# A four-layer graph network: node stages in pairs behind the sums, later hand-overs, the MLP bias by a matmul

## Chip, cores and metric

The kernel runs on one core of a Trainium2 chip. The metric is the device time of one execution in microseconds (us); the median of ten is compared. Engines: PE (TensorE matmuls), PEld (its weight loads), DVE (VectorE), ACT (ScalarE), POOL (GpSimd), SP (SyncE, here only a DMA queue).

## What is computed

A graph of 6250 nodes of 128 features and 100,000 edges (`src`, `dst`) goes through four layers, each on `relu(layernorm(x))`, added to `x`. Cut from the reference:

```python
def layer0(x, ...):                      # attention of 8 heads
    x = layernorm(x) * ln_gamma + ln_beta
    x = x @ W_in + b_in
    e = leaky((x @ W_u + b_u)[src] + (x @ W_v)[dst])
    probs = softmax of e over the edges of one dst
    return segment_sum(x.reshape(n, 16, 8)[src] * probs, dst) @ W_ff + b_ff
def layer1(x, W, b, gamma, beta):        # graph convolution, self loops
    out = segment_sum((x @ W)[src] * dinv[src] * dinv[dst], dst) + b
    return relu(batchnorm over the nodes of out)
def layer2(x, ...):                      # two attention layers of one head, self loops, relu between
    h = x @ W
    e = leaky((h @ a_src)[src] + (h @ a_dst)[dst])
    return segment_sum(h[src] * softmax(e), dst) + bias
def layer3(x, rbf, d_gamma, ...):        # pairs
    w = silu(rbf @ rad_W1 + b) @ rad_W2 + b + silu(d_gamma @ sph_W1 + b) @ sph_W2 + b
    alpha = sum over a head of q[dst-side] * w * k / sqrt(32), times two edge weights
    return segment_sum(alpha * v[...], src)
```

## The kernel before

`survey` sorts the nodes by degree and puts them into 49 blocks (`NR`) of 128; block `b` has room for `CAPS[b]` edges a node (44, 25, 24 ... 9; 820 in all, `TC`). A stage of a layer fetches, for each block, `CAPS[b]` columns: each is one indirect DMA that POOL issues (`fetch`, L1577), 128 rows of a table in HBM, one to a partition. Row tiles have three buffers. Then the block is scored, multiplied and summed on DVE, and the sums go through PE as nodes: transposed, copied by ACT, multiplied with a weight, and written by SP into the table of the next layer. A layer's first gather needs the last of these writes.

From line L1559 on the order on each engine is the order in which the program issues (a manual schedule); nothing is reordered, and an instruction that waits holds all behind it on its engine. The order comes from generators: each `yield` ends a hop, and `in_turns` steps all live blocks once a turn, the older first. A block starts with its gathers, then has `turns_of(b)` turns, about one for 4.5 gathers and at least 4. After each turn `behind` gives background generators a step when their `Pace` says so (a rate per column of `CAPS`):

- layer 0 (`block0`, stage g0): `source_ranks` (the place of each edge's source, 5 columns a step) and `edge_weights` (the MLP of layer 3 over all edges, 200 groups of 500 edges, two hops each: L1236 adds its bias from PSUM and SBUF);
- layer 1 (`part1`): `source_places` (a counting sort, with the scan L1397), and `edge_weights` further; then the batch norm's sums and `blocks1`, 17 groups of three blocks, with no gathers;
- layer 2 (`block2`, stages g2 and g3): the rest of `edge_weights`, then `source_rows` (the rest of the sort: L1447 and L1449 on DVE, L1441 on PE, L1433 on ACT, L1429 on DVE).

The DVE lines of a block: in g0 L1594 to L1598 (scores), L1603 (rows times weights, both in SBUF), L1605 (sum), L1606 to L1609; in g2 and g3 L1745 to L1748, L1753, L1755, L1756 to L1758. The nodes of g0 follow in the same generator: `times_in_hops` with `wf`, L1614 and L1615, `norm_in_hops` (L1045 to L1057), `times_in_hops` with `w1`, L1619. In g3 L1770, the norm, one `times_in_hops` (L1774 and L1775 take it up), then `pair_rows`: POOL fetches the block's edge rows (`pr_e`, L1792, two buffers), DVE multiplies them (L1797, both in SBUF), SP writes them out with `v` (L1801, L1802). `fast_pairs` is the last stage.

Of the kernel before, what the change touches and what calls it, by code (L numbers as in the profile page):

```python
# [842 lines left out]
def survey(k, dst):  # L843
# [9 lines left out]
    with tc.tile_pool(name="sv", bufs=1) as p:  # L853
# [99 lines left out]
        nc.vector.tensor_copy(k.rank_b, rl)  # L953
# [119 lines left out]
def times_in_hops(k, p, ps, h, w, width, got):  # L1073
# [3 lines left out]
    t = ps.tile([128, 512], F32, name="th_p").rearrange("p (b d) -> p b d", b=4)  # L1077
    for b in range(nb):
        nc.tensor.transpose(t[:, b, :], h[:, b, :], k.ident)
    yield  # L1080
# [3 lines left out]
    y = ps.tile([128, 512], F32, name="th_p")  # L1084
# [3 lines left out]
    yield  # L1088
# [102 lines left out]
def edge_weights(k, c, ps, m, bias, attr32, attr4, ew1, ew2):  # L1191
# [39 lines left out]
    def outputs(y, out, n, v):  # L1231

        if v == 0:
            nc.scalar.copy(out[:, :, D:D + 2], scale[:, n * KC:(n + 1) * KC, None].to_broadcast([EP, KC, 2]))
        o = out.rearrange("p (u v) f -> p u v f", v=4)[:, :, v, 0:D]
        nc.vector.tensor_tensor(o, y[:EP].rearrange("p (u d) -> p u d", u=4), bias[:EP, None, :].to_broadcast([EP, 4, D]), op=ALU.add)  # L1236
        if v == 3:
            at = n * KC * (D + 2)
            by_engines(nc.sync.dma_start, to[:, at:at + KC * (D + 2)], out.rearrange("p c f -> p (c f)"))
# [5 lines left out]
    yield  # L1245
    aT = keep(t, 0)
    yield
    t = turn(0, 1)
    yield
    dT = keep(t, 1)  # L1250
    yield
    load(1)
    out = after = None
    g = y = last = None
    for n in range(EC // KC + 1):
        for v in range(4 if n < EC // KC else 1):

            if g is not None:
                y = ps.tile([128, 512], F32, name="ew_y")
                for u in range(4):  # L1260
                    e = slice(u * EP, (u + 1) * EP)
                    nc.tensor.matmul(y[:EP, u * D:(u + 1) * D], lhsT=g[:, 0, e], rhs=m.r2, start=True, stop=False)  # L1262
                    nc.tensor.matmul(y[:EP, u * D:(u + 1) * D], lhsT=g[:, 1, e], rhs=m.s2, start=False, stop=True)  # L1263
            h = None
            if n < EC // KC:
                h = ps.tile([D, 2, 512], F32, name="ew_h")
                nc.tensor.matmul(h[:, 0, 0:4 * EP], lhsT=m.r1[:, v, :], rhs=aT, start=True, stop=True)
                nc.tensor.matmul(h[:, 1, 0:4 * EP], lhsT=m.s1[:, v, :], rhs=dT, start=True, stop=True)
            t = None
            if v in (1, 2) and n + 1 < EC // KC:  # L1270
                t = turn(n + 1, v - 1)
            yield

            gone = last
            if h is not None:
                g = c.tile([D, 2, 4 * EP], F32, name="ew_g", bufs=2)
                for i, first in enumerate((m.b1, m.c1)):
                    nc.scalar.activation(g[:, i, :], h[:, i, 0:4 * EP], AF.Silu, bias=first)  # L1278
            if t is not None:
                new = keep(t, v - 1)  # L1280
                if v == 1:
                    after = new
            if gone is not None:
                if gone[1] == 0:
                    out = c.tile([EP, KC, D + 2], F32, name="ew_out", bufs=2)
                outputs(y, out, *gone)
            last = n, v
            if v == 3:
                aT, dT = after, new
                if n % 2:  # L1290
                    load(n // 2 + 2)
            yield


def source_ranks(k, c, ps):

    nc, tc = k.nc, k.tc
    KC = 5  # L1300
    lanes = k.dram.tile([TC, 128], BF16, name="src_lanes")
# [107 lines left out]
def source_rows(k, c, ps):  # L1409
# [17 lines left out]
    for c0 in range(0, TC + 4 * KS_, KS_):  # L1427
# [8 lines left out]
        for cc, t, l in waiting:  # L1436
            if cc % KG == 0:
                acc = ps.tile([128, 2, 512], F32, name="sr_acc", bufs=2)
# [519 lines left out]
```

## Time and profile before

| what | us |
|---|---|
| median of 10 runs | 6430.18 (6423.03 to 6433.51) |
| the profiled execution | 6431.29, its span 6429.4 |
| POOL, DVE, PE, ACT busy in the span | 4524.6, 4019.6, 2821.1, 1176.2 |
| g0: first gather's start to last gather's end | 450.8 to 1618.0 |
| layer 1's gathers | 1636.4 to 2696.7 |
| g2's gathers | 2777.4 to 3900.7 |
| g3's gathers | 3914.8 to 5163.6 |
| the pairs' gathers and output | 5213.8 to 6425 |
| one gather on POOL: shortest, and idle time behind it | 0.94, 0.30 |

The times of the stages are read from POOL's timeline. A group's row gives busy time and the mean of one instruction, then the idle time of the engine in front of it and what ended it; "issue" there means that the engine waited for nothing the profile shows. An indirect DMA's time on POOL is that of making it, not that of the transfer.

### The profile page before, as it was taken

How to read it: one execution, taken by the hardware profiler on the slowest of the kernel's cores; microseconds unless marked ns; L12 is line 12 of the kernel's file. 1: busy time of each engine (PE TensorE's matmuls, PEld its weight loads, DVE VectorE, ACT ScalarE, POOL GpSimd, SP SyncE). 2: the span in 40 equal slices, each digit the busy share in tenths (PEclk: the TensorE clock that was granted, in tenths of full speed). 3: DMA queues.
4: the chain of work that ended last, by engine and by line, in shares of the span. 5: the costliest groups of instructions: out<-in, count | busy, mean ns of one | idle time of the engine just before them, and what ended most of it. 6: DMA issues, size and time to landing. Idle time of an engine off the chain costs nothing. (4 is left out here: it accounts for less than half of the span.)

```text
span 6429.4 us, 45921 instructions
## 1 busy us (share of the span) xinstructions
PE 2821.1 (44%) x13096; PEld 1851.5 (29%) x13096; DVE 4019.6 (63%) x7548; ACT 1176.2 (18%) x2275; POOL 4524.6 (70%) x4403
## 2 busy tenths in 40 slices
PE   2321444444445456444443443323333136666666
PEld 2211333333223334333321111011111035555555
DVE  9746778885438733443447786667787445555555
ACT  0111233334111111122210010111222211111111
POOL 0047777777677777557777777777777757777776
PEclk9755666766666677666666666656666568888888
DMA  0125334443322223232222223867778853333343
GB/s 6 51 53 87 95 95 104 102 104 81 76 76 73 81 86 92 59 78 78 75 72 50 51 52 47 184 158 178 181 177 183 182 137 100 100 100 101 100 101 91
DMA packets 456941, 626.12 MB, mean 97 GB/s; under 512 B 83151, under 2 KB 357874, under 8 KB 446835
## 3 DMA queue, kind: packets, MB, share of 16 engines
q0 software_dynamic: 159296, 397.56, 25.4%
q1 hardware_dynamic: 297009, 224.87, 15.2%
q8 instruction: 110, 1.80, 0.1%
q14 instruction: 162, 1.33, 0.1%
q10 hardware_dynamic: 364, 0.57, 0.0%
HBM read 441.86 MB, written 180.80 MB: 97 GB/s over the span
## 5 line engine op out<-in xcount | busy, mean ns | idle before, releaser
L1818 POOL DMA_INDIRECT fp_rows<-pair_rows,ids x882 | 863.5, 979 | 288.2 <-issue 201.9
L1577 POOL DMA_INDIRECT g_x<-l2b_t,ranks x776 | 874.4, 1127 | 254.7 <-issue 217.1
L1577 POOL DMA_INDIRECT g_x<-l_t,ranks x820 | 810.4, 988 | 268.1 <-issue 258.7
L1577 POOL DMA_INDIRECT g_x<-l2a_t,ranks x776 | 832.0, 1072 | 236.4 <-issue 227.5
L1577 POOL DMA_INDIRECT g_x<-l_t,ell x776 | 812.6, 1047 | 238.3 <-issue 229.5
L1441 PE MATMUL sr_acc<-sr_t,sr_l 128*128 128x441 f16 x1640 | 527.7, 469 | 987.2 <-DVE sr_l L1449 983.3
L1262 PE MATMUL ew_y<-ew_r,ew_g 128*125 128x128 f32 x1600 | 461.5, 384 | 721.2 <-DVE ew_out L1236 355.3
L1262 PEld LDWEIGHTS ew_y<-ew_r,ew_g 128*125 128x125 f32 x1600 | 365.5, 281 | 787.0 <-ACT ew_g L1278 475.8
L1441 PEld LDWEIGHTS <-sr_l 128*128 128x128 f16 x1640 | 160.3, 116 | 1332.5 <-DVE sr_l L1449 1205.4
L1823 DVE TENSOR_TENSOR fp_oh<-iota_l,fp_rows 128x384 f32<-128x384 f32 x294 | 164.3, 559 | 496.1 <-DMA fp_rows<-pair_rows,ids 495.5
L1849 PE MATMUL fp_acc<-fp_rows,fp_oh 128*128 128x128 f32 x1764 | 333.2, 336 | 280.1 <-DVE fp_rows L1843 279.5
L1263 PE MATMUL ew_y<-ew_s,ew_g 128*125 128x128 f32 x1600 | 451.0, 378 | 5.3
L1656 DVE TENSOR_REDUCE g_s<-g_x 128x128 f32<-128x2432 f32 (+16 forms) x50 | 183.3, 3666 | 382.4 <-DMA g_x<-l_t,ranks 382.4
L1755 DVE TENSOR_REDUCE g_a<-g_x 128x128 f32<-128x2048 f32 (+13 forms) x96 | 389.0, 4052 | 3.3
L1447 DVE TENSOR_SCALAR sr_t<-sr_it,sp_tile 128x882 f16<-128x882 f16 x820 | 383.7, 468 | 0.0
L1263 PEld LDWEIGHTS ew_y<-ew_s,ew_g 128*125 128x125 f32 x1600 | 367.7, 283 | 20.9 <-ACT ew_g L1278 17.8
L1849 PEld LDWEIGHTS fp_acc<-fp_rows,fp_oh 128*128 128x128 f32 x1764 | 271.1, 230 | 353.8 <-DVE fp_rows L1843 353.5
L1797 DVE TENSOR_TENSOR pr_e<-pr_e,pr_kv 128x2432 f32<-128x2432 f32 (+16 forms) x50 | 117.4, 2349 | 353.1 <-issue 178.0
L1831 ACT COPY fp_ot<-fp_tr 128x384 f32<-128x384 f32 x294 | 140.9, 479 | 1071.2 <-PE fp_tr L1828 1062.9
L1835 PE MATMUL fp_qe<-own,fp_ot 128*128 128x128 f32 x1764 | 311.7, 326 | 0.0
L1449 DVE TENSOR_SCALAR sr_l<-sr_it,sp_lane,sr_w 128x128 f16<-128x128 f16 x820 | 299.3, 365 | 11.0 <-POOL sr_w L1419 11.0
L1835 PEld LDWEIGHTS fp_qe<-own,fp_ot 128*128 128x128 f32 x1764 | 286.1, 241 | 0.0
(310 smaller groups left out, 6102.9 us busy)
## 6 DMA issues: line engine op xcount, KB each, us to landing
edge_rows<-ew_out SPq DMA_DIRECT2D x50, 910.0 KB
rk_row<-src_lanes SPq DMA_DIRECT2D x164, 160.0 KB
fp_rows<-pair_rows,ids POOLq DMA_INDIRECT x882
g_x<-l_t,ranks POOLq DMA_INDIRECT x820
g_x<-l_t,ell POOLq DMA_INDIRECT x776
g_x<-l2a_t,ranks POOLq DMA_INDIRECT x776
g_x<-l2b_t,ranks POOLq DMA_INDIRECT x776
ew_a<-in_edge_attr_dram SPq DMA_DIRECT2D x25, 448.0 KB
```

The lines of the kernel that those rows point to most:

```text
L1262: nc.tensor.matmul(y[:EP, u * D:(u + 1) * D], lhsT=g[:, 0, e], rhs=m.r2, start=True, stop=False)
L1263: nc.tensor.matmul(y[:EP, u * D:(u + 1) * D], lhsT=g[:, 1, e], rhs=m.s2, start=False, stop=True)
L1441: nc.tensor.matmul(acc[:, h, 0:HT], lhsT=l, rhs=t[:, h * HT:(h + 1) * HT], start=(cc % KG == 0), stop=end)
L1447: nc.vector.tensor_scalar(t, it, k.tile3[:, cc:cc + 1], None, op0=ALU.is_equal)
L1449: nc.vector.tensor_scalar(l, it[:, 0:128], k.lane3[:, cc:cc + 1], weight[:, cc % KG:cc % KG + 1], op0=ALU.is_equal, op1=ALU.mult)
L1577: nc.gpsimd.indirect_dma_start(out=rows[:, j, :], out_offset=None, in_=table, in_offset=bass.IndirectOffsetOnAxis(ap=ids[:, at:at + 1], ax ...
L1656: nc.vector.tensor_reduce(s, rows[:, :n, :].rearrange("p w d -> p d w"), axis=AX.X, op=ALU.add)
L1755: nc.vector.tensor_reduce(a, v.rearrange("p w d -> p d w"), axis=AX.X, op=ALU.add)
L1818: nc.gpsimd.indirect_dma_start(out=rows[:, t, :], out_offset=None, in_=k.pairs, in_offset=bass.IndirectOffsetOnAxis(ap=k.ids[:, at:at + 1] ...
L1823: nc.vector.tensor_tensor(oh, k.iota_l[:, None, :].to_broadcast([128, TG, 128]), rows[:, :, D + 1:D + 2].to_broadcast([128, TG, 128]), op= ...
L1835: nc.tensor.matmul(qe[:, t, :], lhsT=ot[:, t, :], rhs=k.own[:, h, 0:D], start=True, stop=True)
L1849: nc.tensor.matmul(acc, lhsT=oh[:, t, :], rhs=rows[:, t, D + 2:2 * D + 2], start=(t0 + t == 0), stop=(t0 + t == TB - 1))
```

## The change

- `edge_weights`: the bias enters the PSUM sum by a matmul with a row of ones, and ACT copies the result out. One hop a group instead of two; within a hop first ACT's work on what PE made in the hop before, then PE's.
- `source_ranks`: ten columns a group instead of five, and the high part of a rank is stored times 128, so that PE sums both parts and one column a rank comes out; a group takes two hops, each result is taken up later.
- `source_rows`: the matmuls are issued in the step that makes their operands; groups of 15.
- `times_in_hops` may wait two turns instead of one behind each of PE's parts, and use one PSUM tile for both.
- `in_turns` has a second list, `tails`, stepped after the live blocks. The node part of a block becomes a generator of its own that goes there: in g0 and g2 for two blocks at once, in g3 for one.
- `part1` squares on DVE, in the same hop. The rates of the background work change.

```diff
-        nc.vector.tensor_copy(k.rank_b, rl)
+        nc.vector.tensor_copy(k.rank_b[:, 0, :], rl[:, 0, :])
+        nc.vector.tensor_scalar(k.rank_b[:, 1, :], rl[:, 1, :], 128.0, None, op0=ALU.mult)
...
-def times_in_hops(k, p, ps, h, w, width, got):
+def times_in_hops(k, p, ps, h, w, width, got, late=1, space=512):
...
-    t = ps.tile([128, 512], F32, name="th_p").rearrange("p (b d) -> p b d", b=4)
+    both = ps.tile([128, 512], F32, name="th_p")
+    t = both[:, 0:nb * 128].rearrange("p (b d) -> p b d", d=128)
...
-    yield
+    for _ in range(late):
+        yield
...
-    y = ps.tile([128, 512], F32, name="th_p")
+    y = both[:, space:512] if space < 512 else ps.tile([128, 512], F32, name="th_p")
...
-    yield
+    for _ in range(late):
+        yield
...
+    def second(g):
+        y = ps.tile([128, 512], F32, name="ew_y")
+        nc.tensor.matmul(y[:EP, :], lhsT=k.ones[0:1, 0:EP], rhs=bias[0:1, None, :].to_broadcast([1, 4, D]),
+                         start=True, stop=False)
+        for u in range(4):
+            e = slice(u * EP, (u + 1) * EP)
+            nc.tensor.matmul(y[:EP, u * D:(u + 1) * D], lhsT=g[:, 0, e], rhs=m.r2, start=False, stop=False)
+            nc.tensor.matmul(y[:EP, u * D:(u + 1) * D], lhsT=g[:, 1, e], rhs=m.s2, start=False, stop=(u == 3))
+        return y
...
+    h = first(0, aT, dT)
+    load(1)
...
+    yield
...
+        old = g
+        g = None
+        if s < G:
+            g = c.tile([D, 2, 4 * EP], F32, name="ew_g", bufs=2)
+            for i, b in enumerate((m.b1, m.c1)):
+                nc.scalar.activation(g[:, i, :], h[:, i, 0:4 * EP], AF.Silu, bias=b)
+        if t is not None:
+            if v == 1:
+                next_aT = keep(t, 0)
+            else:
+                next_dT = keep(t, 1)
+        if y is not None:
+            on, ov = groups[s - 2]
+            if ov == 0:
+                out = c.tile([EP, KC, D + 2], F32, name="ew_out", bufs=2)
+                nc.scalar.copy(out[:, :, D:D + 2], scale[:, on * KC:(on + 1) * KC, None].to_broadcast([EP, KC, 2]))
+            nc.scalar.copy(out.rearrange("p (u v) f -> p u v f", v=4)[:, :, ov, 0:D], y[:EP].rearrange("p (u d) -> p u d", u=4))
+            if ov == 3:
+                at = on * KC * (D + 2)
+                by_engines(nc.sync.dma_start, to[:, at:at + KC * (D + 2)], out.rearrange("p c f -> p (c f)"))
+
+        y = second(old) if old is not None else None
+        t = turn(n + 1, v) if v < 2 and n + 1 < EC // KC else None
+        if s + 1 < G:
...
-                aT, dT = after, new
...
+                aT, dT = next_aT, next_dT
+            h = first((v + 1) % 4, aT, dT)
+        if v == 3 and n % 2:
+            load(n // 2 + 2)
+        yield
...
-    KC = 5
+    KC = 10
...
+    starts = list(range(0, TC, KC))
+    made, oh, ob = [], None, None
+    for g in range(len(starts) + 3):
+        if g >= 3:
+            at = slice(starts[g - 3], starts[g - 3] + KC)
+            pr = c.tile([128, KC, NR], F32, name="rk_pr")
+            nc.vector.tensor_tensor(pr, made.pop(0), ob, op=ALU.mult)
+            r = c.tile([128, KC], F32, name="rk_r")
+            nc.vector.tensor_reduce(r, pr, axis=AX.X, op=ALU.add)
+            nc.vector.tensor_tensor(k.ranks[:, at], r, none[:, at], op=ALU.add)
+        if oh is not None:
+            y = ps.tile([128, KC, NR], F32, name="rk_y")
+            for j in range(KC):
+                for n in range(2):
+                    nc.tensor.matmul(y[:, j, :], lhsT=oh[:, j * 128:(j + 1) * 128], rhs=k.rank_b[:, n, :], start=(n == 0), stop=(n == 1))
+            made.append(y)
+        yield
+        oh = None
+        if g < len(starts):
+            oh = c.tile([128, KC * 128], BF16, name="rk_oh")
+            nc.vector.tensor_scalar(oh, rows.pop(0), own, None, op0=ALU.is_equal)
+            rows.append(loaded(starts[g] + 2 * KC))
+        if 2 <= g < len(starts) + 2:
             ob = c.tile([128, KC, NR], F32, name="rk_ob")
...
+                                    hi[:, starts[g - 2]:starts[g - 2] + KC, None].to_broadcast([128, KC, NR]), op=ALU.is_equal)
...
+    KG, KS_ = 15, 3
...
+    for n in range(steps + 4):
...
-        for g, y in full:
+        if full and full[0][0] <= n - 2:
+            _, g, y = full.pop(0)
             f = c.tile([128, 2, HT], F32, name="sr_f")
             nc.scalar.activation(f, y[:, :, 0:HT], AF.Identity, bias=row[:, g:g + 1])
             ready.append((y, f))
...
+        here = range(n * KS_, min((n + 1) * KS_, TC))
+        if here:
+            t = c.tile([128, KS_, TT], F16, name="sr_t", bufs=2)
+            l = c.tile([128, KS_, 128], F16, name="sr_l", bufs=2)
+            for i, cc in enumerate(here):
+                nc.vector.tensor_scalar(t[:, i, :], it, k.tile3[:, cc:cc + 1], None, op0=ALU.is_equal)
+                nc.vector.tensor_scalar(l[:, i, :], it[:, 0:128], k.lane3[:, cc:cc + 1], weight[:, cc % KG:cc % KG + 1],
+                                        op0=ALU.is_equal, op1=ALU.mult)
...
-def in_turns(starts, turns, behind):
+def in_turns(starts, turns, behind, tails=None):
 
 
 
     live = []
+    tails = [] if tails is None else tails
+
+    def hops(lines):
+        return [x for x in lines if step(x)]
...
         for turn in range(turns(b)):
-            new = live[-1:]
-            old = live[:-1]
-            done = [x for x in old if not step(x)]
             if turn == 0:
+                new, live = live[-1:], hops(live[:-1])
+                tails[:] = hops(list(tails))
                 behind(b)
-            done += [x for x in new if not step(x)]
-            if turn:
+                live += hops(new)
+            else:
+                live = hops(live)
+                tails[:] = hops(list(tails))
                 behind(b)
-            live = [x for x in live if x not in done]
         live.append(line)
-    while live:
-        live = [x for x in live if step(x)]
+    while live or tails:
+        live = hops(live)
+        tails[:] = hops(list(tails))
...
+            tails, sums = [], {}
+
+            def nodes0(b, a):
+                nb = a.shape[1]
+                y, h = [], []
+                xb = xp[:, b:b + nb, 0:D]
+                nc.vector.tensor_tensor(xb, xb, bf[:, None, :].to_broadcast([128, nb, D]), op=ALU.add)
+                yield from times_in_hops(k, p, ps, a, wf, D, y, 2, 256)
+                nc.vector.tensor_tensor(xb, xb, y[0], op=ALU.add)
+                yield from norm_in_hops(k, p, xb, h)
+                yield from times_in_hops(k, p, ps, h[0], w1, D, y, 2, 256)
+                o = own[:, b:b + nb, 0:D]
+                nc.vector.tensor_tensor(o, y[1], dinv[:, b:b + nb, None].to_broadcast([128, nb, D]), op=ALU.mult)
+                by_rank(k, t1[0:NP, :], o, b, nb)
+
...
-                a = p.tile([128, 1, D], F32, name="g0_a")
-                nc.vector.tensor_reduce(a[:, 0, :], rows[:, :n, 0:D].rearrange("p w d -> p d w"), axis=AX.X, op=ALU.add)
+                if b % 2 == 0:
+                    sums[b // 2] = p.tile([128, min(2, NR - b), D], F32, name="g0_a")
+                a = sums[b // 2][:, b % 2, :]
+                nc.vector.tensor_reduce(a, rows[:, :n, 0:D].rearrange("p w d -> p d w"), axis=AX.X, op=ALU.add)
...
+                if b % 2 or b == NR - 1:
+                    tails.append(nodes0(b // 2 * 2, sums[b // 2]))
...
-            names = Pace(ranks, 0.3)
+            names = Pace(ranks, 0.22)
...
-                    back.pace = Pace(back.weights, 0.17, 3, NR - 1)
+                    back.pace = Pace(back.weights, 0.07, 3, NR - 1)
...
-            in_turns([block0(b) for b in range(NR)], turns_of, behind)
+            in_turns([block0(b) for b in range(NR)], turns_of, behind, tails)
...
-                d = p.tile([128, 2, D], F32, name="g1_d", bufs=2)
+                d = p.tile([128, 2, D], F32, name="g1_d", bufs=1)
                 nc.vector.tensor_tensor(d[:, 0, :], a, shift, op=ALU.subtract)
-                yield
-                nc.scalar.activation(d[:, 1, :], d[:, 0, :], AF.Square)
-                yield
+                nc.vector.tensor_tensor(d[:, 1, :], d[:, 0, :], d[:, 0, :], op=ALU.mult)
...
-            back.pace = Pace(back.weights, 0.24, 0, NR - 1)
+            back.pace = Pace(back.weights, 0.15, 0, NR - 1)
...
-        back.pace = Pace(back.weights, 0.24)
+        back.pace = Pace(back.weights, 0.14)
...
+                tails, sums = [], {}
+
+                def nodes2(b, a, p, ps):
+                    nb = a.shape[1]
+                    y = []
+                    h = p.tile([128, nb, D], F32, name="g2_h")
+                    nc.scalar.activation(h, a, AF.Relu)
+                    yield
+                    yield from times_in_hops(k, p, ps, h, w3, D + 2, y, 2)
+                    nc.vector.tensor_copy(own[:, b:b + nb, :], y[0])
+                    by_rank(k, t3[0:NP, :], own[:, b:b + nb, 0:D + 1], b, nb)
...
+                def nodes3(b, a, p, ps):
+                    h, y = [], []
+                    xb = xp[:, b, 0:D]
+                    nc.vector.tensor_tensor(xb, xb, a[:, 0, :], op=ALU.add)
+                    yield from norm_in_hops(k, p, xp[:, b:b + 1, 0:D], h)
+                    yield from times_in_hops(k, p, ps, h[0], w4.rearrange("p a d -> p (a d)"), 3 * D, y)
+                    kv = p.tile([128, 2, D], F32, name="pr_kv", bufs=3)
+                    nc.scalar.copy(own[:, b, 0:D], y[0][:, 0, 0:D])
+                    nc.scalar.copy(kv, y[0][:, 0, D:3 * D].rearrange("p (a d) -> p a d", a=2))
+                    yield from pair_rows(k, p, kv, b)
+
...
-                    a = p.tile([128, D], F32, name=name + "_a")
+                    two = 2 if name == "g2" else 1
+                    if b % two == 0:
+                        sums[b // two] = p.tile([128, min(two, NR - b), D], F32, name=name + "_a")
+                    a = sums[b // two][:, b % two, :]
                     nc.vector.tensor_reduce(a, v.rearrange("p w d -> p d w"), axis=AX.X, op=ALU.add)
...
+                    if b % two == two - 1 or b == NR - 1:
+                        tails.append((nodes2 if name == "g2" else nodes3)(b // two * two, sums[b // two], p, ps))
+
+                in_turns([block2(b, name, table, bias, p, bigs, ps, tails, sums) for b in range(NR)], turns_of, behind2, tails)
```

## Prediction

> **What bounds the kernel now.** I read the page's busy times, then the costliest groups, then the windows by stage, then POOL's and DVE's timelines side by side.
>
> ```profile
> PE 2821.1 (44%) x13096; PEld 1851.5 (29%) x13096; DVE 4019.6 (63%) x7548; ACT 1176.2 (18%) x2275; POOL 4524.6 (70%) x4403
> ```
>
> POOL is busiest, but 70% looks like slack. The groups say that it is not:
>
> ```profile
> L1577 POOL DMA_INDIRECT g_x<-l2b_t,ranks x776 | 874.4, 1127 | 254.7 <-issue 217.1
> L1577 POOL DMA_INDIRECT g_x<-l_t,ranks x820 | 810.4, 988 | 268.1 <-issue 258.7
> L1577 POOL DMA_INDIRECT g_x<-l2a_t,ranks x776 | 832.0, 1072 | 236.4 <-issue 227.5
> L1577 POOL DMA_INDIRECT g_x<-l_t,ell x776 | 812.6, 1047 | 238.3 <-issue 229.5
> ```
>
> Nearly all idle time before a gather is "issue": it waits for nobody. In POOL's timeline a gather takes 0.944 us and the gap behind it 0.305 us; every stage goes at 1.249 us a gather. The windows are the five gather stages (layer 0, layer 1, the two halves of layer 2, the pairs), from first to last gather; columns after the colon are length, then PE, PEld, DVE, ACT, POOL busy with their instructions, clock, DMA share, GB/s:
>
> ```profile
> 450.80:1618.00 1167.20, 494.44 (x2401) 341.20 (x2401) 886.82 (x1805) 355.04 (x556) 900.79 (x869) 0.64 0.41 96
> 1636.40:2696.70 1060.30, 555.09 (x2138) 360.08 (x2138) 518.28 (x597) 154.09 (x312) 810.56 (x821) 0.71 0.30 81
> 2777.40:3900.70 1123.30, 496.51 (x1785) 254.54 (x1783) 648.37 (x1183) 182.12 (x368) 873.82 (x822) 0.67 0.27 64
> 3914.80:5163.60 1248.80, 350.77 (x1080) 122.86 (x1078) 848.48 (x1621) 244.10 (x492) 962.41 (x866) 0.61 0.76 167
> ```
>
> Layer 0: 869 x 1.249 = 1085 us of 1167, and the rest is gathers that took longer than 0.944: 81 us. Likewise 37 us in layer 1, 100 us in g2, 145 us in g3. So the time is a fixed count of gathers, plus what holds a gather up, plus the hand-overs between stages (18, 81, 14 and 20 us). Neither PE nor ACT is in it, and DVE only by what holds POOL. This is what holds it (POOL, then DVE, in g3):
>
> ```profile
> 4585.50 0.94 POOL L1577 DMA_INDIRECT g_x<-l2b_t,ranks  x1 [0.30 <-issue]
> 4586.75 3.06 POOL L1577 DMA_INDIRECT g_x<-l2b_t,ranks  x1 [0.30 <-issue]
> 4590.11 2.16 POOL L1577 DMA_INDIRECT g_x<-l2b_t,ranks  x1 [0.30 <-issue]
> 4592.58 0.95 POOL L1577 DMA_INDIRECT g_x<-l2b_t,ranks  x1 [0.31 <-issue]
> ```
> ```profile
> 4586.43 2.56 DVE L1797 TENSOR_TENSOR pr_e<-pr_e,pr_kv 128x2304 f32<-128x2304 f32 x1 [6.90 <-issue]
> 4588.91 2.55 DVE L1753 TENSOR_TENSOR g_x<-g_x,g_e 128x2304 f32<-128x2304 f32 x1
> 4591.50 4.22 DVE L1755 TENSOR_REDUCE g_a<-g_x 128x128 f32<-128x2304 f32 x1
> ```
>
> A gather that begins beside a DVE multiply of two SBUF tiles ends 0.81 us after the multiply (4589.81 after 4588.99); the 4.22 us reduce holds nothing. Each such multiply of length d costs POOL d - V, where V is the time from its start until the next gather is 0.13 us old. If phases are unrelated V averages half of 1.249, 0.62. Measured V: L1603 (layer 0) 0.80; L1753 in g2 1.00 behind L1236 (12 blocks), 0.67 behind L1766 (6), 0.33 behind the sorting's L1449 (29); L1797 0.78; and L1753 in g3 **1.33 in 39 blocks**, because there it starts right behind L1797: the gather that L1797 just let go needs 0.81 + 0.30 + 0.13 us before it can be held again. That neighbourhood is worth 0.7 us a block.
>
> **The change part by part.**
>
> *Bias by matmul (L1236 gone).* 200 DVE additions, 137 us, become 200 PE matmuls (nearest row L1268, 16 x 500 f32, 0.68 us: 136 us) and 200 ACT copies (nearest rows L1228, 500 columns, 0.55, and L1278, 0.67: about 120 us). Hardly a gather is seen held by an L1236 (3 of 200 end just behind one; an operand is PSUM), so DVE's relief buys nothing; PE has 495 to 555 us of work in stages of 1060 to 1167 and covers the cost, ACT likewise (154 to 355). Without that cover the two would be 256 us. Bounds -1 to +2, taken 0. On ACT the copy stands ahead of a later block's Exp; rows have three buffers, so microseconds of lateness reach nobody.
>
> *Ranks in tens.* 164 groups become 82, L1343 goes, 49 rank columns come summed. DVE loses about 27 us (L1343), half of L1339 and L1341 (109 us), half of L1344, and fixed cost of L1353 and L1336: some 150 us, all beside gathers. What counts is one operand pair in SBUF: L1336 held gathers for 2.6 us in 164 at 0.41 us; twice as wide it is the size of L1339 (0.67), and loss goes with d squared: 2.6 x (0.67/0.41)^2 / 2 = 3.5, so **+1**. Bounds 0 and, by unrelated phases (a hold of length d shorter than the period of 1.249 costs d^2 / (2 x 1.249) on average), 82 x 0.67^2 / 2.5 = 15.
>
> The Trainium skill speaks against this part: "SBUF — State Buffer", section "SBUF: two separate sides", has VectorE in a two-port mode lock GpSimd out for the whole instruction, and L1353 is a bf16 one-source operation that doubles in width. By that rule, with its row's 0.38 us against an estimated 0.71, it would go from 164 x 0.38^2/2.5 = 9.5 to 16.5 us, +7; but in this trace L1353 holds one gather in 164, for 0.1 us, so the row gives 0.
>
> *Node stages in pairs behind the sums, layer 0.* Fewer, wider small operations, off POOL's path. But tails now step after the main line: L1603 loses L1614 to L1046 ahead of it. V 0.80 towards 0.62 would be 48 x 0.18 = +8; about half the blocks will instead have a rank comparison just ahead, which helps as L1797 does: taken **+4** (bounds -6, +10). At the end of layer 0 the chain behind the last gather (18.4 us) now shares ACT and DVE with the pair 46/47: two batch norms (0.95) and two Relu (1.0) come in between: **+2.5** (bounds 0, +4). The two later turns are program order alone; with nothing queued they cost no time.
>
> *Layer 1.* Square on DVE: 49 multiplies of 0.29 us; the like L1670 held 0.5 us in all. One hop less before L1690 gains 0.4. Scans and their neighbour L1395 stay. Sum **0**.
>
> *g2.* Weights: 209 steps instead of 407; at 0.07, 0.15 and 0.14 a cap they end at block 12, not 18. So the sorting starts six blocks earlier, and six L1753 go from V 1.00 to 0.33: +4.0. In blocks 0 to 12 nothing of L1236 precedes: their V, 0.78 on average, goes to 0.62: +2.0. Together **+6** (bounds 0, +15). The sorting's matmuls now wait in the same step: PE stands behind DVE up to 2 us, and behind it stand the tails' transposes, read two turns later (one in g3). Nobody on POOL's path.
>
> *g3.* Here the order matters. Old turn: older block's L1797, then L1753. New turn: L1753 and L1755 first, then L1797 with its 7 us wait for pr_e. The 39 pairs part: V 1.33 to 0.62, 0.7 us each. In 22 blocks in full: 15.4. In the 17 others POOL also waited at about its fourteenth gather (0.1 to 1.2 us over the usual 0.3, "DMA g_x") for a gather eight issues back, which the pair rows' stores delay; a hold that falls ahead of that wait is covered by it, one that falls elsewhere is not: half, 6.0. Rows come free about 15 us earlier, as no L1797 wait stands before the reduce: three waits at blocks 42, 43 and 47 go, -2.1 in all. At the end L1797 of block 46 stands behind block 48's sums, 0.4 us sooner than before. Together **+19** (bounds -20, if those waits take in the whole hold, and +40, if V falls to g2's 0.33 in all 39).
>
> Sum: 1 + 4 + 2.5 + 0 + 6 + 19 = **+32.5 us**. The profiled execution took 6431.3 us (span 6429.4 and 1.9 around it); 1.1 above the median 6430.2. So 6464 against the profile, 6462 against the median.
>
> **Rivals.**
> 1. *The holds even out* (20%). DMA waits in g3 take in the parted pairs' cost, V elsewhere stays; the boundary's 2.5 and the comparisons' 1 are left: 6434. For it: phases are accidents, 0.33 to 1.33 in one kernel. Against it: 39 blocks at 1.33 are no accident.
> 2. *Faster: the earlier L1753 is hidden by the DMA* (13%). If 17 of g3's blocks 10 to 35 run at the pace of the stores (0.76 DMA share, against 0.27 to 0.41 before), L1753 falls just ahead of the wait for the eighth-last gather and costs nothing: 17 blocks lose their L1753 hold of about 1.1 us (-19), the row waits go (-2.5), the other parts stay near nothing: 6409. It decides as soon as L1753 ends before the gather that waits; by the steps between (L1797 2.4, sorting 4 x 1.85, small ones 1.9) it would begin 11.7 us after L1797 begins, and the wait before the gather of 4575.05 came 15 us after the L1797 of 4559.6: it is close.
> 3. *A new wait* (7%). The tails hold PSUM banks and small tiles for 14 turns, ACT and PE wait for each other in each weights step; if a DVE instruction waits so long that a row buffer comes late (slack 10 us a block, 3 us at the end), POOL stops: 1 us in each of 2 x 49 blocks, with the forecast's other parts 6560.
> 4. *Not what it says*: the hand-overs from PE that go are no POOL wait in any view; their gain is then zero, which is in the forecast.
>
> **How the numbers follow.** Forecast 60%, at 6462, own range 6444 to 6492. No change here is within 0.2%, 13 us, about what a measurement of this kernel tells from none: 6417 to 6443. Faster 13% (rival 2); same 20% (rival 1); slower 67% (forecast, rival 3). The range 6418 to 6500 leaves out most of rivals 2 and 3.
>
> **What would show it.** Right: gathers still 0.944 + 0.305; V of L1753 in g3 near 0.6 with its row no longer behind L1797; g3's window longer by 10 to 25 us, g2's by about 6, layer 0's by about 5; idle before gathers still "issue"; DVE busy down by 250 to 300 us with no gain. Wrong: gathers' idle put down to DVE or SP, V in g3 above 1, or a changed first-gather gap of a stage by over 5 us.

## The result and the profile after

The changed kernel takes 6638.12 us (median of 8 runs, 6633.43 to 6643.62), 1.0326 of the kernel before [1.0317, 1.0335]: 208 us slower where 32 were forecast, and outside the range of 6418 to 6500. Its profiled span is 6631.4 us, 202.0 more than before.

The page's busy times first, then the stages' windows as before (columns: length, then PE, PEld, DVE, ACT, POOL with their instructions, PE's clock, DMA share, GB/s):

```profile
PE 3282.7 (50%) x14316; PEld 2052.5 (31%) x14316; DVE 3736.5 (56%) x6683; ACT 1157.4 (17%) x2249; POOL 4582.6 (69%) x4403
```
```profile
450.60:1635.40 1184.80, 485.62 (x2931) 313.95 (x2931) 667.90 (x1054) 274.10 (x432) 919.95 (x869) 0.58 0.35 90
1653.80:2730.30 1076.50, 853.22 (x2526) 517.48 (x2526) 473.35 (x549) 207.65 (x394) 816.96 (x821) 0.67 0.31 82
2965.70:4087.90 1122.20, 593.06 (x1883) 278.28 (x1881) 683.66 (x1300) 167.13 (x329) 872.69 (x822) 0.67 0.26 62
4101.30:5363.70 1262.40, 304.46 (x905) 102.33 (x903) 800.25 (x1453) 239.18 (x494) 995.40 (x866) 0.58 0.74 165
```

DVE is 283 us less busy, as forecast, and nothing came of it. PE went the other way, from 2821 to 3283 us, and in layer 1 from 555 to 853. The stages themselves grew little: layer 0 by 18 us, layer 1 by 16, g3 by 14, g2 not at all. The loss stands between the second and the third window: 2730.3 to 2965.7, **235 us without a gather, where there were 81**. Stages and this gap (18 + 16 + 155 - 1 + 14) make 202.

The gap in DVE's timeline: it waits for the batch norm's two sums, which PE makes (L1714).

```profile
2736.51 0.42 DVE L1698 TENSOR_TENSOR g_sums<-g_sums,g_d 106x256 f32<-106x256 f32 x1
2891.86 0.43 DVE L1717 TENSOR_SCALAR g_sums<-g_both 128x256 f32<-128x256 f32 x1 [154.93 <-PE g_both L1714]
```

Before, DVE waited 1.31 us here:

```profile
2704.59 0.42 DVE L1693 TENSOR_SCALAR g_sums<-g_both 128x256 f32<-128x256 f32 x1 [1.31 <-PE g_both L1690]
```

What PE does in those 155 us is steps of the MLP's weights, issued during layer 1 and not done by its end; here is one step and the start of the next (PE, then ACT):

```profile
2811.14 2.06 PE L1243 MATMUL ew_y<-b,ones 1*125 1x512 f32 x2 [1.87 <-ACT ew_out L1289]
...
2816.70 1.39 PE L1237 MATMUL ew_h<-ew_aT,ew_r 128*128 128x500 f32 x2
2818.02 1.10 PE L1238 MATMUL ew_h<-ew_dT,ew_s 16*128 16x500 f32 x2
2820.99 2.06 PE L1243 MATMUL ew_y<-b,ones 1*125 1x512 f32 x2 [1.87 <-ACT ew_out L1289]
```
```profile
2819.22 0.68 ACT L1278 ACTIVATE ew_g<-ew_h,ew_b 128x500 f32<-128x500 f32 x1 [8.13 <-PE ew_h L1238]
2819.80 0.67 ACT L1278 ACTIVATE ew_g<-ew_h,ew_c 128x500 f32<-128x500 f32 x1
2820.36 0.58 ACT L1289 COPY ew_out<-ew_y 125x512 f32<-125x512 f32 x1
```

The step is one chain. PE's first layer (L1238) lets ACT's two Silu go, behind them stands ACT's copy of the last result, and only the copy frees the one PSUM bank into which PE's next bias matmul (L1243) writes. PE waits 1.9 to 2.4 us in each round; a step takes 10.2 us on average all through layer 1. The rate, 0.15 steps a column, puts 121 steps into the 1076 us of layer 1, one every 8.8. (The rate is a place in the program's order: a quicker PE may run ahead of it, but all 121 stand before the batch norm's sums.) Of these PE had started 106 (212 records of L1243) when the last gather ended; 15 at 10.3 us are the 155 us.

### The profile page after: what moved, and what is told of

Read it like the earlier page. It is cut to its first block, busy times and chain, and to the rows that moved or that the text cites. A ratio compares the mean times of both kernels' runs of the same rounds, so it can differ in the third digit from the quotient of the medians.

```text
span 6631.4 us, 47020 instructions
## 1 busy us (share of the span) xinstructions
PE 3282.7 (50%) x14316; PEld 2052.5 (31%) x14316; DVE 3736.5 (56%) x6683; ACT 1157.4 (17%) x2249; POOL 4582.6 (69%) x4403
## 3 DMA queue, kind: packets, MB, share of 16 engines
q8 instruction: 120, 1.97, 0.1%
## 5 line engine op out<-in xcount | busy, mean ns | idle before, releaser
L1595 POOL DMA_INDIRECT g_x<-l2b_t,ranks x776 | 907.8, 1170 | 239.9 <-issue 226.1
L1595 POOL DMA_INDIRECT g_x<-l_t,ell x776 | 831.1, 1071 | 236.8 <-issue 232.9
L1243 PE MATMUL ew_y<-b,ones 1*125 1x512 f32 x400 | 393.7, 1083 | 416.0 <-ACT ew_out L1289 416.0
L1247 PE MATMUL ew_y<-ew_r,ew_g 128*125 128x128 f32 x1600 | 524.8, 429 | 0.0
L1247 PEld LDWEIGHTS ew_y<-ew_r,ew_g 128*125 128x125 f32 x1600 | 414.8, 318 | 286.8 <-issue 286.8
L1248 PE MATMUL ew_y<-ew_s,ew_g 128*125 128x128 f32 x1600 | 492.2, 409 | 0.0
L1682 DVE TENSOR_REDUCE g_s<-g_x 128x128 f32<-128x2432 f32 (+16 forms) x50 | 185.2, 3705 | 532.5 <-DMA g_x<-l_t,ranks 532.5
L1248 PEld LDWEIGHTS ew_y<-ew_s,ew_g 128*125 128x125 f32 x1600 | 424.2, 323 | 0.0
L1831 DVE TENSOR_TENSOR pr_e<-pr_e,pr_kv 128x2432 f32<-128x2432 f32 (+16 forms) x50 | 117.3, 2346 | 408.1 <-DMA pr_e<-edge_rows,start_i 371.7
L1278 ACT ACTIVATE ew_g<-ew_h,ew_b 128x500 f32<-128x500 f32 x200 | 135.4, 677 | 1177.8 <-PE ew_h L1238 1177.1
```

Source lines behind the costliest of these rows:

```text
L1243: nc.tensor.matmul(y[:EP, :], lhsT=k.ones[0:1, 0:EP], rhs=bias[0:1, None, :].to_broadcast([1, 4, D]), start=True, stop=False)
L1595: nc.gpsimd.indirect_dma_start(out=rows[:, j, :], out_offset=None, in_=table, in_offset=bass.IndirectOffsetOnAxis(ap=ids[:, at:at + 1], ax ...
L1682: nc.vector.tensor_reduce(s, rows[:, :n, :].rearrange("p w d -> p d w"), axis=AX.X, op=ALU.add)
```

## Experiments

Theory: the gap is this lag, and the rest is what the prediction said, holds of gathers. Rival: the boundary's own work, or the tails, made the gap. A second question became: is a hold real time at all?

On three of the six chips that ran the experiments (the slower kind, below) the kernel before itself took 7457 to 7573 us, and the ratios differ from those on the other three; what was different there is told at the end. The stage times that the reasoning rests on are from the quicker kind, where the kernel before took 6444 to 6472 us. Its own profile is from the chip of the result above, where it took 6430; so a stage's difference of a few us between an experiment and the kernel before can be the chip's, and the ratios, taken on one chip each, weigh more.

**The rate in layer 1 alone.**

```diff
-            back.pace = Pace(back.weights, 0.15, 0, NR - 1)
+            back.pace = Pace(back.weights, 0.12, 0, NR - 1)
```


> The changed kernel with one number changed: the rate of the weights in layer 1 is 0.12 steps a column instead of 0.15. Theory: a step of the weights takes PE and ACT 10.2 us in turn (ACT's two Silu and copy, then PE's bias, second and first matmuls), layer 1 asks for one every 1.29 / 0.15 = 8.6 us, and what PE owes at its end stands in front of the batch norm's sums. At 0.12 one is asked for every 10.8 us, so nothing is owed: the gap between layer 1's last gather and g2's first falls from 235 us to 75 to 95, DVE's 61 us wait for PE in the sort's start goes (5 us of POOL), and the time to 6475 to 6495. Rival (the gap is the boundary's own work, made longer by the square on DVE or by another order of hops): the gap stays over 200 and the time over 6620.

> The same kernel as e1_pace12 (rate of the weights in layer 1 at 0.12), once more: on the chip of the first four runs the kernel before itself took 7558 us, and ACT and DVE often began an instruction 10 to 60 us after what it waited for was done, so a step of the weights took what the stalls made of it. Theory, for a chip where the kernel before takes 6430 us: gap before g2 75 to 95 us, time 6475 to 6495. Rival (the gap is the boundary's own work): gap over 200 us, time over 6620. On a chip with those stalls: about 1.058 of the kernel before again.

The first ran on a chip of the slower kind and missed: 1.058, a gap of 490 us. The second, on the quicker kind: 6491 us, 1.0067 [1.005, 1.0084], the gap 80.6 us. A step still takes 10.2 us; only less is asked for. With 0.03 less in one rate the ratio falls from 1.0326 to 1.0067, some 165 us, and the boundary's own work, which is the same in both, has no part in that.

**The bias matmul left out.**

```diff
-        nc.tensor.matmul(y[:EP, :], lhsT=k.ones[0:1, 0:EP], rhs=bias[0:1, None, :].to_broadcast([1, 4, D]),
-                         start=True, stop=False)
...
```


> The changed kernel without the bias matmul; the bias of the second MLP layer is left out, ACT still copies the result out. Theory: the step loses the 2.0 us of this matmul and takes 8.2 us, under the 8.6 us that layer 1 asks for: gap before g2 75 to 95 us, time 6475 to 6495. Rival (the copy on ACT, or the one hop a group in which PE and ACT wait for each other, is what made the step long): the step stays over 9.5 us, the gap over 150 us, the time over 6560.

The second layer's first matmul then starts the sum, and the result lacks its bias. The time is inconclusive: it ran only on a chip of the slower kind (1.0403, a gap of 545 us), where late starts (the last section) stretched 20 of layer 1's steps to more than 12 us. But the 52 steps in its gap follow one another without a late start, and there a step takes 8.4 us on average (the theory said 8.2), against 10.2 in the gap of e1 on the same chip. One of them, on PE:

```profile
3417.59 1.10 PE L1238 MATMUL ew_h<-ew_dT,ew_s 16*128 16x500 f32 x2
3420.57 0.79 PE L1245 MATMUL ew_y<-ew_r,ew_g 128*125 128x128 f32 x2 [1.87 <-ACT ew_out L1287]
...
3425.94 1.41 PE L1238 MATMUL ew_h<-ew_dT,ew_s 16*128 16x500 f32 x2
```

So the bias matmul is 1.8 us of the step. PE's wait for ACT is still there, and the granted clock is still 0.69 in this gap.

**ACT's copy ahead of the Silu.**

```diff
         old = g
         g = None
+        if y is not None:
+            on, ov = groups[s - 2]
...
         if s < G:
             g = c.tile([D, 2, 4 * EP], F32, name="ew_g", bufs=2)
...
-        if y is not None:
-            on, ov = groups[s - 2]
...
         y = second(old) if old is not None else None
```


> The changed kernel with ACT's copy of the second layer's result ahead of its two Silu instead of behind them. The result has one PSUM bank, so PE's next second layer waits for the copy, which stood behind the Silu, which waits for PE's first layer. Theory: the 1.9 to 2.4 us that PE waited for ACT in each step go, the bias matmul stays: step 8.0 to 8.4 us, just under the 8.6 asked for, gap before g2 75 to 100 us, time 6475 to 6500. If PE's work alone is too long at the clock granted (over 8.6 us a step) the gap shrinks only in part, to 100 to 160 us, and the time is 6500 to 6570. Rival (the boundary's own work): no change, 6638.

> The changed kernel with ACT's copy ahead of its two Silu, once more, for a chip without stalls (the kernel before at about 6450 us). Theory: step of the weights 8.0 to 8.4 us instead of 10.2, against 8.6 asked for: gap before g2 75 to 100 us, 40 to 65 us over the kernel before. If PE alone needs over 8.6 us: gap 100 to 160, 65 to 125 us over. Rival (the gap is not the chain's): gap over 200, 190 us over.

On the slower kind of chip 1.004, 1.0048 and 1.0062 in three runs (e3, e3b, e3c), with gaps of 304 to 320 us against 490 for the changed rate there. On the quicker kind (e3d) 6488 us, 1.0028 [1.0017, 1.0039]: gap 81.3 us with the rate of 0.15 kept. The theory held, its size did not: not 8 us a step but **4.9**. PE's timeline there:

```profile
2204.32 1.02 PE L1243 MATMUL ew_y<-b,ones 1*125 1x512 f32 x2
...
2207.55 1.01 PE L1237 MATMUL ew_h<-ew_aT,ew_r 128*128 128x500 f32 x2
2208.49 1.10 PE L1238 MATMUL ew_h<-ew_dT,ew_s 16*128 16x500 f32 x2
2209.43 1.02 PE L1243 MATMUL ew_y<-b,ones 1*125 1x512 f32 x2
```

No wait is left, and the bias matmul takes 1.02 us instead of 2.06. The reason shows in the clock column of two 100-us windows in layer 1, the changed kernel's first, then this one's:

```profile
2300.00:2400.00 100.00, 80.19 (x240) 48.49 (x238) 27.37 (x34) 18.35 (x36) 75.62 (x81) 0.67 0.31 90
```
```profile
2100.00:2200.00 100.00, 100.00 (x487) 58.86 (x486) 77.10 (x73) 42.42 (x77) 78.86 (x70) 1.00 0.38 110
2400.00:2500.00 100.00, 0.00 (x0) 0.00 (x0) 26.63 (x31) 0.00 (x0) 75.67 (x80) 0.50 0.20 53
```

With the wait PE is granted 0.67 (in the trace: 3.4 us at full clock, 6.8 at half, again and again, 10.2 in all, the length of the step); without it 1.00 without a break for 433 us, after which it has run ahead to the end of layer 1's steps and has nothing left to do. The wait of 1.9 to 2.4 us cost 5.3 a step.

The Trainium skill ("TensorE: Matmul & The Clock Gate", sections "What's actually happening" and "Why this matters for your kernels") has a window of 3.4 us, two clocks, full and half, and a rule of thumb of no idle gap over about 3 us. The two clocks and the 3.4 us agree with the trace; the rule of thumb is too wide for it, since 1.9 to 2.4 us in every 10.2 were enough.

**All of the change but the weights.** `edge_weights` and its rates as in the kernel before.

```diff
-                    back.pace = Pace(back.weights, 0.07, 3, NR - 1)
+                    back.pace = Pace(back.weights, 0.17, 3, NR - 1)
...
-            back.pace = Pace(back.weights, 0.15, 0, NR - 1)
+            back.pace = Pace(back.weights, 0.24, 0, NR - 1)
...
-        back.pace = Pace(back.weights, 0.14)
+        back.pace = Pace(back.weights, 0.24)
```


> The changed kernel with the weights of the kernel before (DVE adds the bias, two hops a group) and their old rates 0.17, 0.24, 0.24; all else of the change stays. Theory: the whole of the lag is the weights' part; what is left over the kernel before is layer 0's 18 us (one-hots of the ranks 10, phase of the rows' multiply 6, and some), about 7 in layer 1 and 14 in g3: 6455 to 6475, gap before g2 78 to 84 us. Rival (the tails or the later hand-overs hold PE and cause part of the lag): gap over 100 us, time over 6490. Rival (the rest of the change is worth nothing): 6425 to 6440.

> The same kernel as e4_old_weights (weights and rates of the kernel before, the rest of the change kept), once more. Theory, for a chip where the kernel before takes 6430 us: layer 0 +18, layer 1 +7, g3 +14: 6455 to 6475, gap before g2 78 to 84 us. Rivals: gap over 100 us and time over 6490 (tails part of the lag); 6425 to 6440 (the rest is worth nothing). On a chip with stalls: about 0.985 of the kernel before again.

6465 us, 1.0031 [1.0018, 1.0044] on the quicker kind of chip: gap 80.4, layer 0 1178 us, layer 1 1058, g2 1116, g3 1277. So the tails and the later hand-overs have no part in the lag, and layer 1's 16 us, too, were the weights'. On the slower kind 0.9849: there this part of the change takes 1.5% off.

**The ranks in groups of five besides.** `source_ranks` and its rate of the kernel before, on top of e4.

> The changed kernel with the weights (and their rates) and the ranks in groups of five of the kernel before; what is left of the change in layer 0 is the node stages in pairs behind the sums. Theory: the one-hots of ten columns (128x490, both operands in SBUF, 0.66 us) cost the gathers 12.8 us in e4b and go back to about 2.5; the rows' multiply costs 74 to 82: layer 0's stage 1164 to 1171 us instead of 1177, time 4 to 14 us under e4b_old_weights, 5 to 15 us over the kernel before. Rival (the wide one-hots only take the place of other holds): stage 1175 to 1180.

It ran only on the slower kind of chip (0.9847, no different from e4's 0.9849 there), so its stage time says nothing; the gathers held by the one-hots of the ranks can still be counted: 2.2 us, against some 10 with tens in e4 on the same chip (12.8 in e4b). The 10 us are more than half of layer 0's growth.

**g3's node generators ahead of the live block,** on top of e4.

```diff
+                if ahead:
+                    tails[:] = hops(list(tails))
                 live = hops(live)
-                tails[:] = hops(list(tails))
+                if not ahead:
+                    tails[:] = hops(list(tails))
```


> e4b_old_weights with one order changed: in g3 the node generators are stepped ahead of the live block instead of behind it, so that the pair rows' multiply stands right ahead of the next block's multiply again, as in the kernel before. Theory: the gather that was just let go can't be held again for 1.3 us, so g3's rows' multiply costs 60 to 70 us of gathers instead of 103, g3's stage 1245 to 1255 us instead of 1277, time 20 to 32 us under e4b, within 12 us of the kernel before. Rival (g3 grew by something else, the earlier sort or the DMA waits): stage over 1268.

> e4b with g3's node generators stepped ahead of the live block, once more, for a chip without stalls. Theory: the rows' multiply stands right behind the pair rows' multiply again and costs 60 to 70 us of gathers instead of 103: g3's stage 1245 to 1255 us instead of 1277, within 12 us of the kernel before. Rival (the earlier sort or the DMA waits): stage over 1268.

6460 us on the quicker kind, 0.998 [0.997, 0.9991]: a little under the kernel before on that chip, 0.0051 under e4b by ratios from two chips. (On the slower kind 0.9844 and 0.9853, e6 and e6b.) g3 came to 1269 us, a miss (1245 to 1255 was expected): the order did not bring the neighbours back. Only 2 of 49 rows' multiplies stand right behind a pair rows' multiply, at V 1.33 both times, as before; 33 stand behind the sorting at 0.58. Their holds cost 87 us instead of 103 and the DMA waits 20 instead of 9.

**The second operand in PSUM,** on the kernel before.

```diff
-                    nc.scalar.activation(e, e, AF.Exp, bias=s[:, 0:1])
+                    x = es.tile([128, 512], F32, name=name + "_ex")[:, 0:n]
+                    nc.scalar.activation(x, e, AF.Exp, bias=s[:, 0:1])
+                    e = x
...
-        nc.vector.tensor_tensor(e[:, 0:m, 0:D], e[:, 0:m, 0:D], kv[:, 0:1, :].to_broadcast([128, m, D]), op=ALU.mult)
+        nc.vector.tensor_tensor(e[:, 0:m, 0:D], e[:, 0:m, 0:D], by.to_broadcast([128, m, D]), op=ALU.mult)
```


> The kernel before, with the second operand of the three large multiplies in PSUM instead of SBUF: ACT's Exp writes the attention weights of layers 0 and 2 to a PSUM bank, and the pair rows are multiplied with the projection where PE left it; the ranks' PSUM tile has one buffer to make room. Nothing is taken out of the computation. Theory: a gather is held up only by a DVE instruction that reads two operands from SBUF (the bias addition and the ranks' product, each with one operand in PSUM, held next to none), so the holds go: 76 us in layer 0, 96 in g2, 63 and 72 in g3, less what DMA waits take back in g3: 190 to 310 us under the kernel before. Rival (it is the length of a DVE instruction, or its write to SBUF, that holds): within 20 us of the kernel before, or slower by the longer multiply.

On the slower kind of chip 1.0001, a miss in time, and yet the holds are gone: gathers over 0.944 us sum to 3.6 us in layer 0, 5.8 in g2, 9.7 in g3. The time they gave back went into waits for row buffers there (448 us in layer 0). p2_psum_all, with the scan's zeros and a factor of the pairs' multiply in PSUM as well, was 1.0038 there.

> The same kernel as p2_psum_all, once more, for a chip without stalls: is the sum of the holds real time there? Theory (stage = gathers times 1.249 us plus holds plus waits): layer 0 1085 to 1095 us, layer 1 1024 to 1035, g2 1024 to 1035, g3 1085 to 1180, pairs 1155 to 1175, 220 to 350 us under the kernel before. Rival (waits for the DMA semaphores take the place of the holds): within 100 us of the kernel before. On a chip with stalls: 1.0 of the kernel before again.

**6136 us, 0.9484 [0.9455, 0.9514]**, on the quicker kind (two runs): layer 0 1093, layer 1 1046 (more than expected, see the last section), g2 1027, g3 1167, pairs 1165 us. POOL, then DVE, in g3, to be laid beside the lines of the kernel before in the prediction:

```profile
4200.14 0.94 POOL L1577 DMA_INDIRECT g_x<-l2b_t,ranks  x1 [0.30 <-issue]
4201.38 0.94 POOL L1577 DMA_INDIRECT g_x<-l2b_t,ranks  x1 [0.30 <-issue]
4202.63 0.94 POOL L1577 DMA_INDIRECT g_x<-l2b_t,ranks  x1 [0.30 <-issue]
4203.88 0.94 POOL L1577 DMA_INDIRECT g_x<-l2b_t,ranks  x1 [0.30 <-issue]
```
```profile
4199.53 2.69 DVE L1805 TENSOR_TENSOR pr_e<-pr_e,th_p 128x2432 f32<-128x2432 f32 x1 [4.25 <-issue]
4202.14 2.81 DVE L1761 TENSOR_TENSOR g_x<-g_x,g_ex 128x2560 f32<-128x2560 f32 x1
```

The same two multiplies, as long for their width as they were, and none of the gathers beside them is longer. In g3 77 us of waits come out from under the holds (23 before), 56 of them for DMAs. Over all stages the holds fell from 402 us to 49 and the waits rose by 55: some 300 us, against 290 between the two profiled spans and 333 between the medians on p2b's own chip. A hold is real time. The Trainium skill ("SBUF — State Buffer", section "Who interferes with whom") says that a VectorE instruction with two SBUF inputs contends with a GpSimd instruction that reads SBUF, and that one with at most one SBUF input, outside the two-port modes, does not contend with GpSimd: the run agrees, 0.94 us against 2.16 and 3.06. The page also infers that such a multiply does not stall DMAs by way of their descriptors; these gathers were held all the same, and no run shows at which part of making them.

**Both together.** The nodes' part of the change with these operands in PSUM, then all of the change but the ranks, with the copy first:

> The changed kernel with the weights and the ranks of the kernel before, g3's node generators ahead of the live block, and the operands in PSUM of p2_psum_all (the attention weights of layers 0 and 2, the projection that multiplies the pair rows, the zeros of the scan, the factor of the pairs' last multiply). Nothing is taken out of the computation. Theory: gathers are held by two-SBUF-operand DVE instructions alone, so with these gone each stage is its count of gathers times 1.249 us and the waits between: layer 0 1085 to 1095 us, layer 1 1024 to 1040, g2 1024 to 1035, g3 1085 to 1180, pairs 1155 to 1175; where the kernel before takes about 6440 us 6090 to 6220. Rival (waits for the DMA semaphores take the place of the holds): over 6350. On a chip with the stalls the row buffers set the time: 0.97 to 1.0 of the kernel before, gathers still without holds.

> The whole change except the ranks in groups of ten, mended: ACT's copy ahead of its Silu, g3's node generators ahead of the live block, and the operands in PSUM of p2b_psum_all. Nothing is taken out of the computation. Theory: with the holds and the lag gone, where DVE's instructions stand no longer matters, so it takes what p2b took, 0.948 of the kernel before, within 0.006. Rival (the later hand-overs are worth something once the holds are gone): under 0.940. Rival (tails behind cost row buffers or DMA waits): over 0.956. On a chip with stalls: 1.0 to 1.03 of the kernel before.

q1 ran on the slower kind: 1.0113 (a miss, 0.97 to 1.0 was expected), with holds of 5 us or so a stage but 27 in layer 1. r1, on the quicker: 6146 us, 0.9538 [0.9519, 0.9556], just inside what was expected: layer 0 1099, layer 1 1069, g2 1030, g3 1148 us. With holds and lag gone the change gains nothing over p2b.

| kernel | us | kernel before there | ratio |
|---|---|---|---|
| e1b, e4b (one chip) | 6491, 6465 | 6446 | 1.0067, 1.0031 |
| e3d, e6c (one chip) | 6488, 6460 | 6472 | 1.0028, 0.998 |
| p2b; r1 | 6136; 6146 | 6469; 6444 | 0.9484; 0.9538 |
| e1, e2, e3, e4 (slower kind) | 7996, 7860, 7589, 7440 | 7558 | 1.058, 1.0403, 1.004, 0.9849 |
| e3b, e5, e6, p1 (slower kind) | 7594, 7444, 7443, 7564 | 7559 | 1.0048, 0.9847, 0.9844, 1.0001 |
| p2, e6b (slower kind) | 7602, 7453 | 7573 | 1.0038, 0.9853 |
| q1, e3c (slower kind) | 7536, 7506 | 7457 | 1.0113, 1.0062 |

## Why the prediction was wrong

The direction was right and so was the frame (a count of gathers, holds, hand-overs between stages): p2b shows it, with some 300 us taken off by holds alone. **The step that failed is the first, "Bias by matmul", taken at 0 with bounds of -1 to +2: it cost 155 us in the gap and about 16 in layer 1.** Three errors lie in it.

- *The cover.* "PE has 495 to 555 us of work in stages of 1060 to 1167 and covers the cost" looks at PE's sum. PE and ACT take turns within a step, so the question was a step's length against the rate. The trace of before has all of it: 7.6 us of step (2205.49 to 2213.09, PE's wait of 0.9 for ACT included), and with the forecast's own 0.68 for the matmul and 0.6 for the copy 8.9, already over the 8.7 that 0.15 asks for in 1060 us. The old rate, 0.24 of half groups, asked for a group every 10.9. One division would have shown a lag, though by these prices only of some 25 us. The two ends of the 7.6 us, on PE:

```profile
2205.49 0.76 PE L1262 MATMUL ew_y<-ew_r,ew_g 128*125 128x128 f32 x2 [10.25 <-DVE ew_out L1236]
...
2213.09 0.46 PE L1262 MATMUL ew_y<-ew_r,ew_g 128*125 128x128 f32 x2 [0.92 <-ACT ew_g L1278]
```

- *The price.* The row of L1268, 0.68 us, counts two records for each matmul (x400 for 200 groups; its busy time says 1.13). L1243 took 393.7 us, 1.97 each, against 136 forecast; at full clock it is 1.02. With 1.97 in place of 0.68 the same sum gives 10.2, the step as measured.
- *The clock.* Half of the step goes with the wait: 1.9 to 2.4 us are the wait itself, the rest comes of the granted clock, 0.67 with it and 1.00 without it (e3d, 4.9 us). No view of before showed a step without a wait for long enough, so this part could be bounded (busy time at 0.5 and at 1.0), not read.

Who pays was missed too: the batch norm's sums stand behind the weights on PE, at a place where no gather can be issued. The text looked behind each waiting instruction for row buffers; it is the last program-order customer of PE that counts. Rival 3 named "ACT and PE wait for each other in each weights step", but let POOL pay 1 us a block through row buffers, 98 us in all; its condition, a row buffer that comes late, was met once, for 4.9 us (POOL behind DVE's L1682). The forecast's own sign of being wrong did come: a first-gather gap changed by over 5 us, from 81 to 235.

The other terms, by e4b and the changed kernel (e4b's stages are from another chip than those of the kernel before):

- *Ranks, +1:* the wide one-hots (L1363) cost 12.6 us instead of 2.6, +10. The value by unrelated phases, 15, was the better one: L1336's few holds were its phase, and a wider instruction in another place does not keep it. The doubled L1353 (now L1359), put at 0 by its row and at +7 by the skill's rule, held gathers for 2.8 us.
- *Layer 0's multiply, +4; its end, +2.5:* 75.9 to 81.7 us, +6; in e4b and e6c 74 and 76, so none that lasts; the hand-over to layer 1 is 18.4 us as before.
- *Layer 1, 0:* right without the weights (e4b 1058, before 1060).
- *g2, +6:* -1 in the changed kernel, where V is 0.51 behind the sorting (36 blocks), not 0.33, and -7 in e4b. The 0.33 was a phase too.
- *g3, +19:* +14. The pair parted as forecast (none left behind L1831; V 0.33 in 28 blocks, 0.75 in 20), the holds grew by 33 us, more than the 27 of 39 x 0.7, and the DMA waits gave back 19 of 23, more than the 8 allowed for.

Without the weights the forecast's sum stands at 32 (26 without g2's 6, which came of the new weights' earlier end) against 19 measured by e4b's ratio, 12 to 28 by its interval: there the mechanism was right and sizes off.

## What to carry to other kernels

A background stream that runs beside a saturated engine has a rate and a step: divide before trusting busy shares, and where two engines take turns within a step, take the length of the round, with both. Then look at who is last in program order behind that stream on its engine, for there the lag is paid at once. And where a GpSimd queue of indirect DMAs is the bound, give the long DVE multiplies beside it an operand in PSUM before their order is tuned: 5% here, where all the order in this change was worth less than 0.5%.

## What the runs showed of the hardware

- A wait of 1.9 to 2.4 us in each 10.2-us round holds PE at a granted clock of 0.67; without it the clock is 1.00 and the round 4.9 us.
- An operand in PSUM frees the gathers of nearly all holds (402 us to 49). With the scans' zeros there, COPY_PREDICATED beside the gathers of layer 1, of which 0.1 us at most was seen in e4b, takes 21 us in p2b and 37 in r1.
- On three chips ACT and DVE often began instructions long after what they waited for was done. Here, in layer 1 of e1_pace12, PE's matmul ends at 3055.93 and the Silu that needs it starts 61 us later (PE, then ACT):

```profile
3054.83 1.10 PE L1238 MATMUL ew_h<-ew_dT,ew_s 16*128 16x500 f32 x2
```
```profile
3117.37 0.68 ACT L1278 ACTIVATE ew_g<-ew_h,ew_b 128x500 f32<-128x500 f32 x1 [69.91 <-remote]
```

  By the trace's semaphore records the signal of this matmul is marked at 3117.29, 0.08 us ahead of the Silu (in e1b, on another chip, such a signal is marked 0.02 us behind its matmul): what came late is PE's signal, not ACT's answer to it. In each profile on these three chips 97 to 156 such signals for ACT and 104 to 229 for DVE, nearly all of them from PE, came more than 2 us late, 0.85 to 1.77 ms in sum for either engine; in the profiles on the other chips there is none. Whether PE's work itself ended later than the profile has it, or only its signal, stays open, and so does the cause. The kernel before takes 15% to 18% longer on those chips, and the change without its weights wins 1.5% there where it loses 0.3% on the others. That its fewer and later hand-overs from PE are the reason is likely but not shown, as the kernel before was profiled on none of those chips.
